# Layer 1's biases in its weights, one range check for four windows, logits in four key groups

## The chip, the cores and the metric

The kernel runs on one core of one Trainium2 chip. The metric is the device time of that core in microseconds, the median of several executions. The core has a matmul engine (TensorE, PE in the profile; PEld is its weight load), three engines for elementwise work (VectorE or DVE, ScalarE or ACT, GpSimd or POOL) and SyncE (SP), which here only issues DMA transfers. Matmuls read on-chip memory (SBUF) and write banks of PSUM, 128 partitions by 512 fp32 values, of which there are eight.

## The reference, cut to what matters

An image batch x of 4 x 128 channels x 64 x 64 goes through two layers.

```python
# layer 0, in windows of 16 x 16 pixels, BR = 2 branches, 4 heads of 32 channels
y = layernorm2d(x); y = y + depthwise_3x3(y)
q, k, v = (einsum('ncij,bhdc->nbhdij', windows(y), M) for M in (Wq, Wk, Wv))
logits = einsum('nbhdij,nbhdkij->nbhkij', q, patches_5x5(k)) * 32 ** -0.5   # zero padded
o = einsum('nbhkij,nbhdkij->nbhdij', softmax(logits, axis=3), patches_5x5(v))
x = x + unwindowed((Wo[0] @ o[0] + 0.5 * Wo[1] @ o[1]) / sqrt(1.25))

# layer 1, on tokens t: 4 x 4096 x 128
z = ln(t) @ W.T + b                     # W is 384 x 128; q, k, v are its thirds
q, k, v = elu(z_q) + 1, elu(z_k) + 1, z_v
t = t + (q . cumsum(k v^T)) / (q . cumsum(k) + 1e-6)
w = batchnorm(ln(t) @ Wf.T)
y_s = sigmoid(w_s + y_{s-1} @ V.T)      # a scan along the 4096 tokens
x = t + y
```

`ln` has no gain and no offset, so its output sums to zero over the 128 channels.

## The kernel before

The image is cut into 16 bands (4 images, 4 bands of 16 rows), a band into four windows, which makes 64 windows. The main loop (L708) walks one slot per window, with two slots more to drain. In slot i it writes, in this order: `logits` of window i, `scaled` (the division by the softmax sums) of window i-2, `weighted` of window i-1 (sums, values, inverse, in three steps) and `window_inputs` (q, k, v) of window i+1, in three steps. Between these stand six gaps (`between(i, 0)` to `between(i, 5)`); each takes one step of `behind`, the layer-1 work of a finished band (`layer1`, 24 steps in the list at L621, so one band of layer 1 per four slots), and in most slots one of `ahead`, the normalisation and depthwise convolution of a coming band. `in_order` (L161) fixes the order of PE, DVE, ACT and POOL to the written one; the SP queue takes its transfers in the order in which the Tile scheduler puts them, and a transfer into a buffer comes after the buffer's release. All PSUM tiles of this stage share eight banks.

**logits** (L371). For each head, a bank holds 128 key slots (partitions) by 512 queries (two branches of 256). A bf16 product of `mask_k` and `mask_q` (L379) first writes 0 or -1e30, then `BLOCKS` (L27) splits the queries into rows 0 to 6, 6 to 10 and 10 to 16, each with its own eight rows of keys (from rows 0, 4 and 8), in two halves of 64 key slots: 2 branches x 3 blocks x 4 heads x 2 halves = 48 products at L391, each with 32 rows (channels of the head) by 64 columns (keys) of the array, so eight tiles of it hold the 4 heads and 2 halves. ACT takes the exponentials `es` out of the banks (L400).

**weighted** (L403). A product with ones (L409) gives the sums `den`, and a transfer packs them into `dc` of 128 x 16; the values product (L421) uses `v_sb`, whose middle third is put together from the outer two by two transfers within SBUF (L360, L361). DVE adds the padding's share (L432), inverts (L434) and keeps a running maximum and minimum of the sums (L435, L436). These are compared with 1e-30 and 1e30 at the end (L876 to L879). If a sum left the range, or the recurrence's check failed, the program branches to `general`, another version of the whole computation.

**layer1** works on half bands of 512 tokens (16 x 2 of them). `turn` (L496) transposes the normalised tokens into `xl`. `feature` (L500), for q and for k, multiplies by a third of `awT`, takes exp(z + b) on ACT (L505), the minimum of this and 1 on DVE (L507) and then max(z + b + 1, that) on DVE (L508). `values` (L517) multiplies by the last third and adds `abv`, the bias spread over all partitions, on DVE (L528).

**prepare** (L134) runs once on DVE after the first convolutions and scales `woT`. After the main loop the recurrence (L823) runs 41 rounds and writes the output.

Of the kernel before, what the change touches and what calls it, by code (L numbers as in the profile page):

```python
# [9 lines left out]
F32 = mybir.dt.float32  # L10
BF16 = mybir.dt.bfloat16
AF = mybir.ActivationFunctionType
# [5 lines left out]
P = 128  # L18
# [5 lines left out]
BR, HEADS, HD = 2, 4, 32  # L24
KR = 2
KC = 64
BLOCKS = ((0, 6, 0), (6, 10, 4), (10, 16, 8))  # L27
BAND = WS * W
# [7 lines left out]
WARM = 11  # L36
TOL = 5e-7
TINY, HUGE = 1e-30, 1e30

# [8 lines left out]
def conv_attn_hybrid(ctx: ExitStack, tc: tile.TileContext, ins: dict, out: bass.AP):  # L48
# [75 lines left out]
    awT = loaded("awT", [P, 3 * P])  # L124
    ab = loaded("ab", [P, 3])
    abv = loaded("abv", [P, P], src=ins["abv"].partition_broadcast(P))
    fwT = loaded("fwT", [P, P])
# [3 lines left out]

    ab1 = const.tile([P, 2], F32, name="ab1")

    def prepare():  # L134


        rect = math.sqrt(1.0 + LAM * LAM * (BR - 1))
        nc.vector.tensor_scalar(woT[:, 0], woT[:, 0], 1.0 / rect, None, ALU.mult)
        nc.vector.tensor_scalar(woT[:, 1], woT[:, 1], LAM / rect, None, ALU.mult)
        nc.vector.tensor_scalar(ab1, ab[:, :2], 1.0, None, ALU.add)  # L140


    dmax = const.tile([P, 16], F32, name="dmax")
    nc.vector.memset(dmax, 1.0)
    dmin = const.tile([P, 16], F32, name="dmin")
    nc.vector.memset(dmin, 1.0)

# [32 lines left out]
    def run(g):  # L180
        for _ in g:
            pass
# [148 lines left out]
    def window_inputs(w, n, wj):  # L331
# [27 lines left out]

        nc.sync.dma_start(v_sb[:64, 1, :], v_sb[64:, 0, :])  # L360
        nc.sync.dma_start(v_sb[64:, 1, :], v_sb[:64, 2, :])  # L361
        w["v"] = v_sb
# [3 lines left out]

    def spans(br, n):
        r0, r1, key0 = BLOCKS[n]
        return slice(br * WT + r0 * WS, br * WT + r1 * WS), br * WT + key0 * WS

    def logits(w):  # L371
# [3 lines left out]
        for h in range(HEADS):  # L375
            rows = slice(h * HD, (h + 1) * HD)

            for c in range(0, P, KC):
# [6 lines left out]
                )  # L385
        for br, n in pieces:
            cols, k0 = spans(br, n)
            for h in range(HEADS):
                rows = slice(h * HD, (h + 1) * HD)
                for c in range(0, P, KC):  # L390
                    nc.tensor.matmul(  # L391
                        sps[h][c : c + KC, cols],
                        w["k"][rows, k0 + c : k0 + c + KC],
                        w["q"][rows, cols],
                        start=False,
                        stop=(br, n) == pieces[-1],
                    )
        for h in range(HEADS):
            es = p2.tile([P, BR * WT], F32, tag=f"es{h}", name=f"es{h}")
            nc.scalar.activation(es, sps[h], AF.Exp, scale=scale)  # L400
            w["es", h] = es

    def weighted(w):  # L403
# [8 lines left out]
        nc.scalar.copy(den, dps)  # L412
        dc = p2.tile([P, 16], F32, tag="dc", name="dc")
        nc.sync.dma_start(dc, den[::HD, :])
        yield
        for br, n in pieces:
            cols, _ = spans(br, n)
            for h in range(HEADS):
# [15 lines left out]
        nc.vector.reciprocal(rc, dc)  # L434
        nc.vector.tensor_tensor(dmax, dmax, dc, ALU.max)  # L435
        nc.vector.tensor_tensor(dmin, dmin, dc, ALU.min)  # L436
        rd = dram4.tile([HEADS, BR * WT], F32, tag="rd", name="rd")
# [58 lines left out]
    def turn(h):  # L496
        h.xl = p2.tile([P, 512], F32, tag="xl", name="xl")
        nc.scalar.copy(h.xl, turned(h.xn, 0, 4))

    def feature(h, m):  # L500

        zps = bank()
        nc.tensor.matmul(zps, awT[:, m * P : (m + 1) * P], h.xl, start=True, stop=True)  # L503
        low = p2.tile([P, 512], F32, tag="low", name="low")
        nc.scalar.activation(low, zps, AF.Exp, bias=ab[:, m : m + 1])  # L505
        f = p2.tile([P, 512], F32, tag=f"f{m}", name=f"f{m}")
        nc.vector.tensor_scalar(low, low, 1.0, None, ALU.min)  # L507
        nc.vector.scalar_tensor_tensor(f, zps, ab1[:, m : m + 1], low, ALU.add, ALU.max)  # L508
        return f
# [7 lines left out]
    def values(h):  # L517
        vvps = bank()
        for j in range(4):
# [7 lines left out]
        h.v1 = v1s[h.s]  # L527
        nc.vector.tensor_tensor(  # L528
            h.v1[:, :, :P],
            vvps.rearrange("p (j d) -> p j d", d=P),  # L530
            abv.unsqueeze(1).to_broadcast([P, 4, P]),
            ALU.add,
        )

# [160 lines left out]
    next(third)  # L695
    windows = {0: {}}
    run(window_inputs(windows[0], 0, 0))
# [3 lines left out]
    def between(i, gap):  # L701
# [3 lines left out]
        if i < len(places) and (i == 0 or i % NB or gap in (0, 2, 4)):  # L705
            next(ahead, None)

    for i in range(len(places) + 2):  # L708
        if i < len(places):
            n, wj = places[i]  # L710
            if i and wj == 0 and n + 1 < len(bands) and bands[n + 1][1] < NB - 1:
                load_head(n + 2)
            logits(windows[i])
        if 2 <= i:
            m, wjm = places[i - 2]
            if wjm == NB - 1:
                run(behind)
                behind = layer1(m, halves.pop(m - 1, (None, None)))
        between(i, 0)
        if 2 <= i:  # L720
            scaled(m, wjm, windows.pop(i - 2))
        if i < len(places) and wj == 1 and n + 2 < len(bands):
            load(n + 2)
        sums = weighted(windows[i - 1]) if 1 <= i <= len(places) else iter(())
        for gap in (1, 2):
            next(sums, None)
            between(i, gap)
        run(sums)
        if i == 0:
            run(fourth)  # L730
        inputs = iter(())
        if i + 1 < len(places):
            windows[i + 1] = {}
            inputs = window_inputs(windows[i + 1], *places[i + 1])
        for gap in (3, 4, 5):
            next(inputs, None)
            between(i, gap)
        run(inputs)
    run(behind)
# [119 lines left out]

    NG = 4  # L860
    okc = sp.tile([P, NG + 1], F32, name="okc")
    d = sp.tile([P, COLS], F32, name="d")
# [12 lines left out]

    nc.vector.tensor_scalar(dmax, dmax, HUGE, None, ALU.is_le)  # L876
    nc.vector.tensor_scalar(dmin, dmin, TINY, None, ALU.is_ge)
    nc.vector.tensor_tensor(dmin, dmin, dmax, ALU.mult)
    nc.vector.tensor_reduce(okc[:, NG : NG + 1], dmin, AX.X, ALU.add)  # L879
    okp = ps_m.tile([P, 512], F32, tag="bank", name="bank")  # L880
    nc.tensor.matmul(okp[:1, : NG + 1], ones[:, :1], okc, start=True, stop=True)
    oks = sp.tile([1, 1], F32, name="oks")
    nc.vector.tensor_reduce(oks, okp[:1, : NG + 1], AX.X, ALU.add)
    bad = sp.tile([1, 1], mybir.dt.int32, name="bad")
    nc.vector.tensor_scalar(bad, oks, float(2 * P * B * SEGS + P * 16), None, ALU.is_lt)
    rec.close()
# [591 lines left out]
def _masks():  # L1478
# [10 lines left out]
    pad = np.zeros((1, BR, WT), np.float32)  # L1489
    for r0, r1, key0 in BLOCKS:  # L1490
        for q in range(r0 * WS, r1 * WS):
            r, c = divmod(q, WS)
            for i in range(8):
                queries[:, i, :, q] = 0.0 if abs(key0 + i - r) <= KR else -BIG
            for j in range(WS):
# [60 lines left out]
```

## Time and profile before

| | us |
|---|---|
| median of 3 runs | 928.18 (926.36 to 929.19) |
| the profiled execution | 923.71 |
| its span | 922.0 |
| PE busy | 871.1 (94%) |
| PEld busy | 647.3 (70%) |
| DVE busy | 737.1 (80%) |
| ACT busy | 539.9 (59%) |
| POOL busy | 256.4 (28%) |
| L391, logits: PE busy, 6144 passes | 90.7 |
| L400, exponentials, ACT, x256 | 132.2 |
| L508, feature, DVE, x64 | 48.0 |

An fp32 matmul shows as two passes, each with its own weight load. A pass is counted once per tile of the array, and passes of several tiles run side by side, so that busy time is the union and a mean is not a cost. The span is the time between the first and the last instruction that the profiler saw; the execution's own time has 1.7 us more around it. Times in microseconds from the start of the span are used below to name places.

### The profile page before, as it was taken

To read this page: it belongs to the slowest core of one execution; us is meant where nothing else is said; L and a number is where in the kernel's file an instruction comes from. 1 tells how busy PE (TensorE), PEld (TensorE's weight loads), DVE (VectorE), ACT (ScalarE), POOL (GpSimd) and SP (SyncE) were. 2 spreads that over 40 slices of the span, in tenths; PEclk is the share of its full clock that TensorE was granted. 3 is DMA by queue.
4 is the path that set the end of the run, shared out by engine and by line. 5 is a ranking of instruction groups with operands and counts; after the bars stand their busy time and mean duration, and the time that the engine had idled before them with its cause. 6 is when DMAs were issued, how large, how long until landed. Compare 5 with 4: busy or idle time off the path is not lost.

```text
span 922.0 us, 33116 instructions
## 1 busy us (share of the span) xinstructions
PE 871.1 (94%) x13836; PEld 647.3 (70%) x13836; DVE 737.1 (80%) x2408; ACT 539.9 (59%) x1010; POOL 256.4 (28%) x358
## 2 busy tenths in 40 slices
PE   4977999999999999999999999999999999978885
PEld 3756777777777877777787777777777778656452
DVE  6464878888898978798888889787978887577695
ACT  3754666565756565665656575656666565522563
POOL 2122131423232232304132323323231412131174
PEclk9989999999999999999999999999999999989798
DMA  4111121122222121212112121212121111110854
GB/s 122 35 46 55 38 79 42 50 58 64 61 64 55 53 57 50 75 38 71 49 50 61 61 60 50 63 50 68 50 72 38 57 39 51 43 37 23 365 212 159
DMA packets 53071, 63.89 MB, mean 69 GB/s; under 512 B 22960, under 2 KB 33840, under 8 KB 52400
## 3 DMA queue, kind: packets, MB, share of 16 engines
q1 hardware_dynamic: 51184, 56.91, 19.8%
q10 hardware_dynamic: 1728, 4.77, 1.3%
q8 instruction: 111, 1.82, 0.8%
q14 instruction: 48, 0.39, 0.1%
HBM read 35.44 MB, written 17.30 MB: 57 GB/s over the span
## 4 chain that ended last, share of the span: by engine, by line
PE 59%; DVE 26%; DMA 4%; ACT 4%; issue 3%; POOL 2%; ACTq 0%; DVEq 0%; SPq 0%; POOLq 0%
DVE y L289 9%; PE bank L338 8%; PE bank L474 7%; PE bank L213 6%; PE bank L391 6%; PE bank L503 5%; PE bank L409 4%; PE bank L351 4%; PE bank L421 3%; PE bank L611 3%; DMA res<-resd 2%; DVE st L192 2%; PE bank L546 2%; PE z L831 2%; DVE state L571 2%
## 5 line engine op out<-in xcount | busy, mean ns | idle before, releaser
L289 DVE SCALAR_TENSOR_TENSOR y<-ypad,cpe_w,y 128x512 f32<-128x512 f32 x240 | 190.1, 792 | 14.5 <-ACT y L287 11.0
L400 ACT ACTIVATE es<-bank 128x512 f32<-128x512 f32 x256 | 132.2, 603 | 64.5 <-PE bank L391 64.5
L449 POOL TENSOR_TENSOR oT<-o_sb,rden 128x512 f32<-128x512 f32 x64 | 85.0, 1328 | 240.0 <-DMA rden<-rd 166.5
L196 POOL TENSOR_SCALAR rs<-mv 128x4 f32<-128x4 f32 (+2 forms) x100 | 25.2, 252 | 366.0 <-DVE mv L194 162.5
L204 DVE TENSOR_SCALAR xn<-x,mv,rs 128x128 f32<-128x128 f32 x256 | 92.5, 422 | 26.6 <-POOL rs L197 26.6
L197 POOL TENSOR_TENSOR rs<-rs,mhalf 128x4 f32<-128x4 f32 (+2 forms) x100 | 106.1, 1061 | 8.3
L391 PEld LDWEIGHTS bank<-q,k 32*64 32x64 f32 x6144 | 89.1, 132 | 4.4 <-ACT k L346 1.8
L391 PE MATMUL bank<-q,k 32*64 32x96 f32 (+1 forms) x6144 | 90.7, 247 | 1.0 <-ACT k L346 1.0
L421 PEld LDWEIGHTS bank<-es,v_sb 128*32 128x32 f32 x3072 | 56.5, 110 | 30.7 <-issue 19.5
L474 PE MATMUL bank<-woT,oT 128*128 128x128 f32 x512 | 67.3, 287 | 7.5 <-POOL oT L449 7.5
L474 PEld LDWEIGHTS bank<-woT,oT 128*128 128x128 f32 x512 | 64.0, 200 | 11.6 <-POOL oT L449 9.2
L421 PE MATMUL bank<-es,v_sb 128*32 128x96 f32 (+1 forms) x3072 | 69.9, 239 | 0.5 <-issue 0.5
L503 PE MATMUL bank<-xl,awT 128*128 128x512 f32 x128 | 70.0, 630 | 0.0
L358 ACT COPY v_sb<-bank 128x512 f32<-128x512 f32 x64 | 37.5, 586 | 54.1 <-PE bank L351 46.0
L409 PE MATMUL bank<-es,ones 128*32 128x512 f32 x512 | 69.0, 611 | 0.0
L338 PE MATMUL bank<-y2w,wqT 128*128 128x256 f32 x256 | 67.0, 385 | 1.0 <-DVE y2w L289 1.0
L338 PE MATMUL bank<-y2w,wkT 128*128 128x256 f32 x256 | 65.8, 380 | 0.0
L351 PE MATMUL bank<-wvT,y2w 128*128 128x256 f32 x256 | 65.8, 380 | 0.0
L346 ACT COPY q<-bank 128x512 f32<-128x512 f32 x64 | 37.6, 587 | 44.2 <-PE bank L338 42.1
L346 ACT COPY k<-bank 128x512 f32<-128x512 f32 x64 | 37.3, 583 | 36.8 <-PE bank L338 36.7
L192 DVE BATCH_NORM_STATS2 st<-x 128x6 f32<-128x128 f32 x256 | 55.5, 279 | 1.1
L338 PEld LDWEIGHTS bank<-y2w,wqT 128*128 128x128 f32 x256 | 46.2, 195 | 13.0 <-issue 7.2
(118 smaller groups left out, 1719.6 us busy)
## 6 DMA issues: line engine op xcount, KB each, us to landing
rden<-rd SPq DMA_DIRECT2D x64, 256.0 KB
v_sb<-v_sb SPq DMA_DIRECT2D x128, 64.0 KB
resd<-rs_o SPq DMA_DIRECT2D x32, 256.0 KB
out<-ot SPq DMA_DIRECT2D x32, 256.0 KB
xin<-in_xt SPq DMA_DIRECT2D x15, 512.0 KB
res<-resd SPq DMA_DIRECT2D x2, 2048.0 KB
res<-resd ACTq DMA_DIRECT2D x2, 2048.0 KB
dc<-den SPq DMA_DIRECT2D x64, 8.0 KB
```

What stands on the lines that cost most here:

```text
L197: nc.gpsimd.tensor_tensor(rs[:, :n], rs[:, :n], mhalf[:, :n], ALU.pow)
L204: nc.vector.tensor_scalar(xn[:, j, :], piece, mv[:, j, 0:1], rs[:, j : j + 1], ALU.subtract, ALU.mult)
L289: nc.vector.scalar_tensor_tensor(y2, src, cpe_w[:, tap : tap + 1], y2, ALU.mult, ALU.add)
L338: nc.tensor.matmul(pps[:, br * WT : (br + 1) * WT], wT[:, br * P : (br + 1) * P], y2, start=True, stop=True,)
L351: nc.tensor.matmul(vps[:, e * 256 : (e + 1) * 256], y2[:, e * P : (e + 1) * P], wvT, start=True, stop=True,)
L391: nc.tensor.matmul(sps[h][c : c + KC, cols], w["k"][rows, k0 + c : k0 + c + KC], w["q"][rows, cols], start=False, stop=(br, n) == pieces[-1],)
L400: nc.scalar.activation(es, sps[h], AF.Exp, scale=scale)
L409: nc.tensor.matmul(dps[rows], ones[:, :HD], w["es", h], start=True, stop=True)
L421: nc.tensor.matmul(ops[rows, cols], w["v"][:, n, c0 : c0 + HD], w["es", h][:, cols], start=(br, n) == pieces[0], stop=(br, n) == pieces[-1],)
L449: nc.gpsimd.tensor_tensor(oTs[n][:, :, :, wj * WS : (wj + 1) * WS], w["o"].rearrange("p (a r c) -> p a r c", a=BR, c=WS), w["rden"].rearra ...
L474: nc.tensor.matmul(yps[:, j * P : (j + 1) * P], oT[:, br, t], woT[:, br, :], start=br == 0, stop=br == BR - 1,)
L503: nc.tensor.matmul(zps, awT[:, m * P : (m + 1) * P], h.xl, start=True, stop=True)
```

## The change

Layer 1's biases: `ab` is now all 384 biases, spread over all partitions. `prepare` computes the sums of `awT` over its 128 rows on TensorE, adds 1 to the biases of q and k, and adds (bias - sum) / 128 to every row of `awT`, so that each of its columns sums to the bias. `turn` adds 1 to `xl` while it evicts it. As `ln`'s output sums to zero over the channels, the product then holds z + b (+ 1 for q and k) by itself. `feature` takes exp(that - 1), with a constant column `minus` as bias, and one DVE instruction makes max(min(low, 1), product). `values` evicts with a copy on ACT.

The sums' range: `dc` is a quarter of a tile for four windows. In the fourth window, `in_range` makes two DVE instructions over 64 columns, which count the sums in range into a column of `okc`. `dmax` and `dmin` are gone.

The logits: the middle block's halves hold key rows 8 to 12 and 4 to 8, so the first half of the key slots always holds rows 0 to 4 or 8 to 12 and the second rows 4 to 8 or 12 to 16. Per branch there are two steps instead of three blocks: rows 0 to 4 for queries of rows 0 to 6 beside rows 4 to 8 for 0 to 10, and rows 8 to 12 for 6 to 16 beside rows 12 to 16 for 10 to 16. That is 32 products of 96 or 160 columns. `mask_q` and the transfers of `v_sb`'s middle third follow.

The slot's order is written as a list; what it orders is as before, but for `load` (the band's input transfer), which is now written right behind `logits`, ahead of `between(i, 0)` and `scaled`.

```diff
-BLOCKS = ((0, 6, 0), (6, 10, 4), (10, 16, 8))
+BLOCKS = ((0, 6, (0, 4)), (6, 10, (8, 4)), (10, 16, (8, 12)))
+TILES = (((0, 0, 0, 6), (1, 4, 0, 10)), ((0, 8, 6, 16), (1, 12, 10, 16)))
...
-    ab = loaded("ab", [P, 3])
-    abv = loaded("abv", [P, P], src=ins["abv"].partition_broadcast(P))
+    ab = loaded("ab", [P, 3 * P], src=ins["ab_all"].partition_broadcast(P))
...
-        nc.vector.tensor_scalar(ab1, ab[:, :2], 1.0, None, ALU.add)
+        sums = bank()[:, : 3 * P]
+        nc.tensor.matmul(sums, ones, awT, start=True, stop=True)
+        nc.vector.tensor_scalar(ab[:, : 2 * P], ab[:, : 2 * P], 1.0, None, ALU.add)
+        nc.vector.tensor_tensor(ab, ab, sums, ALU.subtract)
+        nc.vector.scalar_tensor_tensor(awT, ab, 1.0 / P, awT, ALU.mult, ALU.add)
...
-        nc.sync.dma_start(v_sb[:64, 1, :], v_sb[64:, 0, :])
-        nc.sync.dma_start(v_sb[64:, 1, :], v_sb[:64, 2, :])
+        nc.sync.dma_start(v_sb[:64, 1, :], v_sb[:64, 2, :])
+        nc.sync.dma_start(v_sb[64:, 1, :], v_sb[64:, 0, :])
...
-        for br, n in pieces:
-            cols, k0 = spans(br, n)
-            for h in range(HEADS):
-                rows = slice(h * HD, (h + 1) * HD)
-                for c in range(0, P, KC):
-                    nc.tensor.matmul(
-                        sps[h][c : c + KC, cols],
-                        w["k"][rows, k0 + c : k0 + c + KC],
-                        w["q"][rows, cols],
...
+        for br in range(BR):
+            for step in TILES:
+                for h in range(HEADS):
+                    rows = slice(h * HD, (h + 1) * HD)
+                    for half, key, r0, r1 in step:
+                        cols, k0 = span(br, r0, r1), br * WT + key * WS
+                        nc.tensor.matmul(
+                            sps[h][half * KC : (half + 1) * KC, cols],
+                            w["k"][rows, k0 : k0 + KC],
+                            w["q"][rows, cols],
...
+    def in_range(group):
+        found = dens.pop(group).rearrange("p w e -> p (w e)")
+        low = p1.tile([P, DGROUP * 16], F32, tag="low_dc", name="low_dc")
+        nc.vector.tensor_scalar(low, found, HUGE, None, ALU.is_le)
+        nc.vector.scalar_tensor_tensor(
+            low, found, TINY, low, ALU.is_ge, ALU.mult, accum_out=okc[:, NG + group : NG + group + 1]
+        )
...
-        nc.vector.tensor_tensor(dmax, dmax, dc, ALU.max)
-        nc.vector.tensor_tensor(dmin, dmin, dc, ALU.min)
+        if at == DGROUP - 1:
+            in_range(group)
...
-        nc.scalar.copy(h.xl, turned(h.xn, 0, 4))
+        nc.scalar.activation(h.xl, turned(h.xn, 0, 4), AF.Identity, bias=ones[:, :1])
...
-        nc.scalar.activation(low, zps, AF.Exp, bias=ab[:, m : m + 1])
+        nc.scalar.activation(low, zps, AF.Exp, bias=minus)
         f = p2.tile([P, 512], F32, tag=f"f{m}", name=f"f{m}")
-        nc.vector.tensor_scalar(low, low, 1.0, None, ALU.min)
-        nc.vector.scalar_tensor_tensor(f, zps, ab1[:, m : m + 1], low, ALU.add, ALU.max)
+        nc.vector.scalar_tensor_tensor(f, low, 1.0, zps, ALU.min, ALU.max)
...
-        nc.vector.tensor_tensor(
-            h.v1[:, :, :P],
-            vvps.rearrange("p (j d) -> p j d", d=P),
-            abv.unsqueeze(1).to_broadcast([P, 4, P]),
-            ALU.add,
-        )
+        nc.scalar.copy(h.v1[:, :, :P], vvps.rearrange("p (j d) -> p j d", d=P))
```

## The prediction

> **What bounds the kernel now.** I read the busy time of each engine in stretches of 47 us first, because an average over the span mixes three stages.
>
> ```profile
> core 0: us, PE busy (x) PEld busy (x) DVE busy (x) ACT busy (x) POOL busy (x), PEclk, DMA share, GB/s
> ...
> 228.00:275.00 47.00, 46.95 (x791) 35.08 (x790) 40.78 (x140) 28.70 (x52) 12.97 (x19) 1.00 0.18 54
> ...
> 416.00:463.00 47.00, 46.97 (x830) 35.40 (x831) 40.26 (x125) 30.01 (x55) 12.21 (x17) 1.00 0.21 61
> ...
> 792.00:850.00 58.00, 49.28 (x482) 37.58 (x480) 41.12 (x155) 18.61 (x32) 10.99 (x15) 0.94 0.11 36
> 850.00:922.00 72.00, 55.31 (x181) 29.79 (x180) 50.94 (x92) 35.81 (x90) 30.79 (x35) 0.86 0.60 235
> ```
>
> From about 90 to 810 us TensorE is busy 46.9 of every 47 us at the full granted clock, DVE 40, ACT 29. One band of 16 rows takes about 47 us and four slots, so a slot is 11.7 us of TensorE work in the written order. TensorE time saved there comes off the end, as long as DVE and ACT stay under it. From 810 to 850 the last band's layer 1 runs alone, and after 850 the recurrence, which the change leaves as it is.
>
> Next the TensorE timeline of one slot's start and, from the chain of waits, undisturbed groups (start, duration, line; x counts passes, two for each fp32 matmul).
>
> ```profile
> 406.92 0.42 PE L379 MATMUL bank<-mask_q,mask_k 32*64 32x512 bf16 x8
> 407.16 1.39 PE L391 MATMUL bank<-q,k 32*64 32x96 f32 x96
> 408.48 0.49 PE L582 MATMUL bank<-v,aT 128*128 128x129 f32 x2
> ```
>
> ```profile
> 416.85 0.86 PE bank L338 x4
> ...
> 423.98 1.00 PE bank L409 x8
> ...
> 426.47 1.02 PE bank L421 x48
> ```
>
> The logits of a window (L391) hold TensorE from 407.16 to 408.48: 1.32 us. L338 streams 4 passes of 256 columns in 0.86 us, 0.84 ns for a column and pass.
>
> **The logits.** Eight tiles of the array (four heads, two key halves) each stream 2 branches x 256 query columns, twice: 1024 x 0.84 = 0.86 us when all run abreast. This doesn't change: 96+64+96 columns per branch become 96+160 in one half and 160+96 in the other. So 0.46 of the 1.32 us is not streaming. L409 and L421 stream as much in each of their four tiles and take 1.00 and 1.02 us, so some 0.15 us belongs to any such group (the change-over to the next shape), and 0.31 us comes with L391's number of matmuls. It falls from 48 to 32 a window (96 to 64 passes). Bounds: if the 0.31 us shrinks with the count alone, a third goes, 0.10 us; if it vanishes, 0.31 us. I take the count's place between the rows: 48 passes (L421) cost nothing extra, 96 cost 0.31, so 64 keep a third and 0.20 us goes. Over 64 windows: **-12.8 us** (-6.4 to -19.8).
>
> The Trainium skill (TensorE: Matmul & The Clock Gate, "Architectural detail") gives TensorE a queue of 64 instructions. A matmul of two passes is four instructions (two weight loads, two passes), so by that rule a third of a window's 192 can wait in line before, half of 128 after, and weight loads would be fetched ahead more often: a gain nearer the upper bound. No row shows the queue, and the sum doesn't use it.
>
> **DVE's work.** The rows of the groups by form:
>
> ```profile
> L507 DVE TENSOR_SCALAR low<-low 128x512 f32<-128x512 f32 x64 | 27.4, 428 | 26.8 <-ACT low L505 26.7
> L528 DVE TENSOR_TENSOR v<-bank,abv 128x512 f32<-128x512 f32 x32 | 21.9, 683 | 0.7 <-PE bank L520 0.6
> L436 DVE TENSOR_TENSOR dmin<-dmin,dc 128x16 f32<-128x16 f32 x64 | 10.4, 162 | 0.0
> L435 DVE TENSOR_TENSOR dmax<-dmax,dc 128x16 f32<-128x16 f32 x64 | 7.1, 111 | 0.0
> L346 ACT COPY q<-bank 128x512 f32<-128x512 f32 x64 | 37.6, 587 | 44.2 <-PE bank L338 42.1
> ```
>
> Gone: the minimum L507 (27.4; the fused L508 does it in its own 751 ns), the value addition L528 (21.9), the two running extremes (17.5): 66.8 us. New: one range check for four windows, 16 x (two operations on 128x64, taken as 0.25 us each, between the 0.16 us of L436 on 16 columns and the 0.62 us of L866 on 256, and an accumulator read of 0.08 us) = 9 us. Net -57 us, 3.6 us a band: DVE goes from 40 to about 36.5 of the band, now some 46. DVE is not the last to be done in these stretches, so this work is worth only the waits that it ends. TensorE's waits for DVE between 40 and 790 us are 1.9 us at transposes (L213 waiting for x of L596), and 5.4 us in its weight loads there: I take -1.0 us (0 to -5).
>
> In the last band DVE is the chain:
>
> ```profile
> 830.38 0.34 DVE low L507
> ...
> 831.50 0.35 DVE low L507
> ...
> 835.51 0.44 DVE low L507
> ...
> 836.72 0.60 DVE v L528
> ```
>
> These four go: **-1.7 us** (0, if ACT or TensorE is right behind, to -3.1, all four minima of 0.43 and both additions of 0.68). L876 to L879, 0.7 us in all, lie beside TensorE work near 810 us: 0.
>
> **ACT's work.** The values' 32 evictions move to ACT: 32 x 0.59 (row L346, the same copy out of PSUM) = 19 us, and the 32 evictions of `xl` get a bias, 593 to some 690 ns (row L505, 688 ns, an activation with a bias): 3 us. ACT goes from 29 to 30.5 of a band; TensorE's 46 hide it. In a slot they stand at gap 4 (half 0) and gap 3 (half 1), where `k` or `v` of the next window is queued behind; these are needed only at the next slot's logits or later. 0; with the cover gone up to 19 us (a rival below).
>
> **Start.** `prepare` gains a 128x384 product on TensorE (2 x 384 x 0.84 = 0.65 us) and about 1.3 us on DVE (two operations on 384 columns, one on 256, by the 0.79 us of L289 on 512). TensorE is free from 12.36 (the end of L213's 0.47 us from 11.89) to 13.59, where L307 waits for the padded rows, and `awT` has landed by 9.96 us in the packet records. DVE does `prepare` at 22.3 us, the normalised rows that follow have over 2 us of slack before their transposes at 29.69, and then it sits idle 9.24 us until 36.92. Cost 0, with the cover gone +2. The bias row's 192 KB in place of 64 KB has ten us to arrive.
>
> **Queues.** SP issues the same transfers. Its `load` is written ahead of `between(0)` and `scaled`, but the buffer it fills is free only after L481 of the second half, at 433.89 in that slot, and the load leaves at 434.59, behind that window's `rd` and `rden`. It can't go ahead of the `dc` transfer: DVE needs `dc` at 431.30, before that L481, so the two would wait for each other. 0. The two `v_sb` transfers keep bytes and count, and now stay in their own 64 partitions: 0.
>
> Sum: 12.8 + 1.0 + 1.7 = 15.5 us off the profiled execution's span of 922.0 (923.71 with what lies around it), so 906.5 and 908.2. The three timed runs have their median at 928.18, 4.5 above that execution; the same difference carries it to **912.7 us**.
>
> **Rivals.**
> (a) *The unequal halves pace each other.* If matmuls start and end in the written order, a 96-column tile waits for the 160-column one beside it, and every step costs 160: 4 x 160 x 2 x 0.84 = 1.08, with the 0.15 of change-over 1.23 us. Gain 0.09 x 64 = 5.8, with 2.7 from DVE 8.5: 919.7 us. For: all eight tiles now have equal work in every step, so the trace can't show the case. Against: up to 32 of L391's passes touch one tenth of a microsecond, so the tiles overlap freely. Chance 0.17. The Trainium skill (TensorE: Matmul & The Clock Gate, "The mechanism" of Part 3) states this rule: matmuls are strict first in, first out, at start and end. The trace's records carry no tile, so they neither confirm nor refute it.
> (b) *The count is not the cost.* If the 0.31 us is the price of eight row-and-column tiles (as against four), the logits stay at 1.32 us: only 2.7 us go, 925.5. For: no group in this trace has eight fp32 tiles with fewer matmuls. Chance 0.10.
> (c) *Everything beyond streaming goes*: 19.8 + 2.7 = 22.5, 905.7. Chance 0.06.
> (d) *ACT takes the lead; slower.* At gaps 3 and 4 ACT would evict late, a bank come free late and TensorE stand, 0.59 us in each of 32 halves: +19 - 15.5 = +3.4, 931.6. It decides from 0.48 us exposed per half. Against: ACT is idle 18 of 47 us, waiting for TensorE at these very copies (44 us before L346's q). Chance 0.05.
> The forecast keeps 0.62.
>
> The range takes the logits' bounds and DVE's: 22.5 to 27 us off at the low end, 6 to 8 at the high: 902 to 923. It holds the forecast, (a) and (c); (b), (d) and part of the forecast's edges are left out. A run set tells 0.3% (2.8 us, 925.4) from no change; (b) lies on that edge and is split: faster 0.89, same 0.06, slower 0.05.
>
> **What would show it.** After: L391 with 4096 passes, and from its start to the next group's 1.12 us (1.23 for (a), 1.32 for (b), 1.01 for (c)); TensorE still busy 99% from 90 us on, in bands of about 46 us; DVE near 680 us in sum, ACT near 562; no new wait of TensorE for ACT at the banks of L338 or L520 (else (d)); the stretch from 829 to 838 shorter by about 2 us. The prediction is wrong if TensorE shows idle time in the steady bands, whichever engine ends it.

## The result, and the profile after

| | before | after |
|---|---|---|
| median, us | 927.27 (4 runs, 925.18 to 929.19) | 904.72 (4 runs, 902.29 to 906.12) |
| the profiled execution | 923.71 | 903.84 |
| its span | 922.0 | 902.1 |

The ratio of the times is 0.9744, with a 95% interval of 0.9712 to 0.9775 (the two medians divided give 0.9757). The kernel became 22.55 us faster by the medians and 19.9 by the two profiled spans; the forecast was 15.5.

The busy times of the page of after, and then the engines' shares of the chain that ended last, first of after and then of before:

```profile
PE 852.1 (94%) x11790; PEld 634.3 (70%) x11790; DVE 686.5 (76%) x2229; ACT 561.5 (62%) x1042; POOL 256.1 (28%) x358
...
PE 75%; DVE 11%; DMA 5%; ACT 3%; POOL 2%; issue 2%; ACTq 0%; SPq 0%; POOLq 0%; DVEq 0%
```

```profile
PE 59%; DVE 26%; DMA 4%; ACT 4%; issue 3%; POOL 2%; ACTq 0%; DVEq 0%; SPq 0%; POOLq 0%
```

TensorE's share of busy time is 94% in both, but DVE's share of the chain fell from 26% to 11%. The prediction didn't read the shares of the chain; the 26% was the warning that it missed (the share is 27% in e1 below, which keeps DVE's old work, and 9% in e2, which doesn't).

The groups of the page of after that answer to the changed lines (logits; `low`; the fused `f`). Line numbers are those of after: the mask product is L385, the logits L398, the transposes L220, the q product L345, the states L586, x L611, the range check L416 and L417.

```profile
L528 DVE SCALAR_TENSOR_TENSOR f<-low,bank 128x512 f32<-128x512 f32 x64 | 43.6, 682 | 49.5 <-ACT low L526 49.5
...
L398 PE MATMUL bank<-q,k 32*64 32x96 f32 (+1 forms) x4096 | 77.4, 276 | 1.0 <-ACT k L353 1.0
...
L526 ACT ACTIVATE low<-bank,minus 128x512 f32<-128x512 f32 x64 | 44.1, 689 | 19.2 <-PE bank L524 19.2
```

There are 4096 passes in place of 6144. The 49.5 us of idle time before the fused operation will matter below: DVE stands there, waiting for ACT's exponential.

TensorE's timeline of after around one window's logits (start, duration, line, passes):

```profile
397.54 0.42 PE L385 MATMUL bank<-mask_q,mask_k 32*64 32x512 bf16 x8
397.77 1.20 PE L398 MATMUL bank<-q,k 32*64 32x96 f32 x64
398.90 0.49 PE L597 MATMUL bank<-v,aT 128*128 128x129 f32 x2
```

From the logits' start to the next group it is 1.13 us; the median over the steady windows is 1.125, against 1.318 before. That is 0.193 us a window, 12.4 us over 64 windows, where the forecast said 12.8. The rest of the gain is elsewhere. A band is four slots, and the mask product marks where a slot starts. These are the busy times of one band's four slots, before and then after (length of the slot, then each engine's busy time):

```profile
406.92:421.33 14.41, 13.92 (x229) 11.14 (x229) 13.72 (x60) 7.33 (x14) 4.86 (x7) 1.00 0.17 53
421.33:434.66 13.33, 13.33 (x228) 10.74 (x228) 10.42 (x43) 8.31 (x16) 4.20 (x8) 1.00 0.18 53
434.66:446.23 11.57, 11.57 (x193) 7.31 (x193) 9.83 (x27) 7.98 (x15) 3.41 (x3) 1.00 0.31 83
446.23:457.35 11.12, 11.12 (x207) 8.57 (x206) 9.65 (x18) 7.70 (x14) 1.75 (x1) 1.00 0.14 39
```

```profile
397.54:410.68 13.14, 13.14 (x198) 10.93 (x198) 12.23 (x57) 7.31 (x14) 4.87 (x7) 1.00 0.21 61
410.68:423.81 13.13, 13.13 (x195) 10.53 (x194) 10.27 (x41) 8.32 (x16) 4.20 (x8) 1.00 0.18 51
423.81:435.14 11.33, 11.33 (x161) 7.07 (x160) 9.83 (x24) 8.78 (x16) 3.40 (x3) 1.00 0.33 83
435.14:446.07 10.93, 10.93 (x175) 8.38 (x174) 7.44 (x14) 8.18 (x15) 1.27 (x1) 1.00 0.14 39
```

Slots 1, 2 and 3 became 0.19 to 0.24 shorter, which is the logits' share. Slot 0 became 1.27 shorter here. Before, DVE was busy 13.72 of its 14.41 us: it set this slot's length, though over the band it was busy only 43.6 of 50.4. TensorE's timeline shows where it waited in that slot, before and then after:

```profile
412.67 1.16 PE L546 MATMUL bank<-f,f 128*128 128x128 f32 x8
413.67 0.38 PE L213 MATMUL bank<-ident,x 128*128 128x128 f32 x2
414.50 0.59 PE L213 MATMUL bank<-ident,x 128*128 128x128 f32 x2 [0.46 <-DVE x L596]
414.93 1.03 PE L338 MATMUL bank<-y2w,wqT 128*128 128x256 f32 x4
```

```profile
403.10 1.16 PE L561 MATMUL bank<-f,f 128*128 128x128 f32 x8
404.09 0.60 PE L220 MATMUL bank<-ident,x 128*128 128x128 f32 x4
404.53 1.03 PE L345 MATMUL bank<-y2w,wqT 128*128 128x256 f32 x4
```

From the first transpose of x to the q product it took 1.26 us before and takes 0.44 after: 0.82 us of standing, of which the row shows 0.46 as idle. The remainder lies under the transposes' own records and is counted as busy. This is one of the longer waits: over the 12 steady bands (those of the last table below) the stretch took 0.97 us on average before, from 0.59 to 1.40, and takes 0.44 after, so 0.53 us a band is gone here. The Trainium skill (Perfetto Trace Analysis, "Tensor Engine Instruction (MATMUL, LD_WEIGHTS)") says that a TensorE record's end is estimated and not observed; these rows agree, and show how much of a wait that can cover.

Later in the same slot TensorE stands once more, at the transposes of xn, the normalised tokens that DVE writes. Before and then after, DVE's row first:

```profile
419.01 1.11 DVE L204 TENSOR_SCALAR xn<-x,mv,rs 128x128 f32<-128x128 f32 x4
...
419.50 1.00 PE L213 MATMUL bank<-ident,xn 128*128 128x128 f32 x4
420.34 0.39 PE L582 MATMUL bank<-v,aT 128*128 128x129 f32 x2
```

```profile
408.36 1.11 DVE L211 TENSOR_SCALAR xn<-x,mv,rs 128x128 f32<-128x128 f32 x4
...
408.91 0.95 PE L220 MATMUL bank<-ident,xn 128*128 128x128 f32 x4
409.69 0.39 PE L597 MATMUL bank<-v,aT 128*128 128x129 f32 x2
```

Four such passes took 0.44 us at x after; from these to the next product it is 0.84 us before and 0.78 after, on average 0.83 and 0.71, while DVE is still writing xn. No row shows idle time for it. So the changed kernel still stands here for some 0.27 us a band.

The lag can be seen on DVE. Its timeline in the same slot, before and then after; the last rows of after are the range check:

```profile
405.45 0.68 DVE L528 TENSOR_TENSOR v<-bank,abv 128x512 f32<-128x512 f32 x1
...
407.50 1.33 DVE L571 TENSOR_TENSOR state<-state,bank 128x129 f32<-128x129 f32 x4
...
414.10 0.61 DVE L596 SCALAR_TENSOR_TENSOR x<-bank,rd,x 128x128 f32<-128x128 f32 x2
```

```profile
396.28 1.33 DVE L586 TENSOR_TENSOR state<-state,bank 128x129 f32<-128x129 f32 x4
...
402.88 0.61 DVE L611 SCALAR_TENSOR_TENSOR x<-bank,rd,x 128x128 f32<-128x128 f32 x2
...
406.44 0.13 DVE L416 TENSOR_SCALAR low_dc<-dc 128x64 f32<-128x64 f32 x1
406.61 0.23 DVE L417 SCALAR_TENSOR_TENSOR low_dc<-dc,low_dc 128x64 f32<-128x64 f32 x1
406.76 0.08 DVE L417 DVE_READ_ACCUMULATOR low_dc<-dc,low_dc 128x1 f32 x1
```

The state additions started 0.58 us after the slot's mask product before (407.50 against 406.92), and start 1.26 us ahead of it now (396.28 against 397.54). DVE enters slot 0 with 1.8 us less work left over, so x is there when TensorE comes to its transposes.

The whole difference by place, from the starts of the 64 mask products (means over the 12 steady bands; my own sums):

```
             slot 0  slot 1  slot 2  slot 3 | to 13th mask | 48 steady slots | next three | last mask to end | span
before        14.07   13.42   11.53   11.12 |    155.63    |     601.66      |   36.96    |     127.72       | 921.98
after         13.01   13.27   11.33   10.93 |    154.29    |     582.55      |   36.39    |     128.88       | 902.11
difference    -1.06   -0.15   -0.20   -0.19 |     -1.34    |     -19.11      |   -0.57    |      +1.16       | -19.87
```

Of the 19.1 us in the steady slots, 48 x 0.193 = 9.3 is the logits and 9.8 is slot 0 standing less, 0.8 us for each of 12 bands: 0.53 at the transposes of x and 0.26 from the v product ahead of the transposes of xn to the product behind them. This split is by place; what each half of the change is worth by itself is another question, and the experiments answer it.

### The profile page after: what moved, and what is told of

It reads as the page before. It is cut to its first block, busy times and chain, and to the rows that moved or that the text cites. A ratio compares the mean times of both kernels' runs of the same rounds, so it can differ in the third digit from the quotient of the medians.

```text
span 902.1 us, 28877 instructions
## 1 busy us (share of the span) xinstructions
PE 852.1 (94%) x11790; PEld 634.3 (70%) x11790; DVE 686.5 (76%) x2229; ACT 561.5 (62%) x1042; POOL 256.1 (28%) x358
## 4 chain that ended last, share of the span: by engine, by line
PE 75%; DVE 11%; DMA 5%; ACT 3%; POOL 2%; issue 2%; ACTq 0%; SPq 0%; POOLq 0%; DVEq 0%
PE bank L345 11%; PE bank L524 7%; PE bank L495 7%; PE bank L398 6%; PE bank L427 6%; PE bank L220 6%; PE bank L442 6%; PE bank L358 5%; PE bank L561 3%; PE bank L626 3%; PE bank L597 3%; PE bank L540 3%; DVE y L296 3%; DMA res<-resd 3%; PE bank L578 2%; PE bank L599 2%
## 5 line engine op out<-in xcount | busy, mean ns | idle before, releaser
L296 DVE SCALAR_TENSOR_TENSOR y<-ypad,cpe_w,y 128x512 f32<-128x512 f32 x240 | 186.7, 778 | 11.7 <-ACT y L294 7.5
L470 POOL TENSOR_TENSOR oT<-o_sb,rden 128x512 f32<-128x512 f32 x64 | 82.3, 1285 | 229.0 <-DMA rden<-rd 192.7
L211 DVE TENSOR_SCALAR xn<-x,mv,rs 128x128 f32<-128x128 f32 x256 | 94.5, 430 | 28.2 <-POOL rs L204 28.2
L528 DVE SCALAR_TENSOR_TENSOR f<-low,bank 128x512 f32<-128x512 f32 x64 | 43.6, 682 | 49.5 <-ACT low L526 49.5
L398 PEld LDWEIGHTS bank<-q,k 32*64 32x64 f32 x4096 | 75.7, 132 | 4.4 <-ACT k L353 1.8
L398 PE MATMUL bank<-q,k 32*64 32x96 f32 (+1 forms) x4096 | 77.4, 276 | 1.0 <-ACT k L353 1.0
L442 PEld LDWEIGHTS bank<-es,v_sb 128*32 128x32 f32 x3072 | 56.5, 110 | 30.1 <-issue 26.2
L345 PE MATMUL bank<-y2w,wqT 128*128 128x256 f32 x256 | 67.2, 386 | 1.5 <-DVE y2w L296 1.5
L345 PE MATMUL bank<-y2w,wkT 128*128 128x256 f32 x256 | 66.1, 381 | 0.0
L526 ACT ACTIVATE low<-bank,minus 128x512 f32<-128x512 f32 x64 | 44.1, 689 | 19.2 <-PE bank L524 19.2
```

The costliest lines, as they stand in the source:

```text
L211: nc.vector.tensor_scalar(xn[:, j, :], piece, mv[:, j, 0:1], rs[:, j : j + 1], ALU.subtract, ALU.mult)
L296: nc.vector.scalar_tensor_tensor(y2, src, cpe_w[:, tap : tap + 1], y2, ALU.mult, ALU.add)
L345: nc.tensor.matmul(pps[:, br * WT : (br + 1) * WT], wT[:, br * P : (br + 1) * P], y2, start=True, stop=True,)
L398: nc.tensor.matmul(sps[h][half * KC : (half + 1) * KC, cols], w["k"][rows, k0 : k0 + KC], w["q"][rows, cols], start=False, stop=br == BR - ...
L442: nc.tensor.matmul(ops[rows, cols], w["v"][:, n, c0 : c0 + HD], w["es", h][:, cols], start=(br, n) == pieces[0], stop=(br, n) == pieces[-1],)
L470: nc.gpsimd.tensor_tensor(oTs[n][:, :, :, wj * WS : (wj + 1) * WS], w["o"].rearrange("p (a r c) -> p a r c", a=BR, c=WS), w["rden"].rearra ...
```

## The experiments

The expectations use letters. **A**: TensorE sets slots 1 to 3, and DVE's left-over work sets slot 0; so a saving on TensorE is lost in slot 0 as long as DVE is late there, and a saving on DVE is paid in slot 0. **B**: TensorE bounds every slot, and each part is worth what it saves there. **Q**: a matmul of the logits is held up because TensorE holds only so many instructions, which enter in the written order and are freed in order; the eight array tiles themselves run independently of each other. Other letters in them are rivals whose price stands beside them; (a) to (d) are those of the prediction. "Steady slots" are those of the last table.

**Each half of the change by itself.** `e1_logits_only` is the kernel before with the new `BLOCKS`, `TILES`, masks and transfers; `e2_rest_only` is the changed kernel with the 48 products of before.

```diff
 # e1, on the kernel before; e2 is the reverse, on the changed one
-BLOCKS = ((0, 6, 0), (6, 10, 4), (10, 16, 8))
+BLOCKS = ((0, 6, (0, 4)), (6, 10, (8, 4)), (10, 16, (8, 12)))
+TILES = (((0, 0, 0, 6), (1, 4, 0, 10)), ((0, 8, 6, 16), (1, 12, 10, 16)))
...
-        for br, n in pieces:
+        for br in range(BR):
+            for step in TILES:
```

> The kernel before with the logits in 32 products and nothing else. Measured between the two traces: a window's logits took 1.318 us before and 1.125 after, and nearly every slot is 0.19 us shorter, but the first slot of each band (window 0) is shorter by a further 0.9 us; there DVE was busy 13.4 of 14.1 us before. Theory A (DVE sets the end of that slot before): with TensorE 0.19 us quicker in every slot and DVE's work unchanged, TensorE reaches its transposes of x earlier and waits longer; what three of a band's four slots gain is lost in the first slot. The logits take 1.125 us a window, but the kernel gains only 3 to 8 us against before, and slot 0 of a band gets longer by 0.2 to 0.6 us. Theory B (parts add up): 64 x 0.193 = 12.4 us gained.

> The changed kernel with the logits again in 48 products: biases in the weights, values evicted by ACT, range check for four windows. Theory A (DVE's backlog held TensorE in the first slot of each band): these slots lose 0.8 to 0.9 us each, 13 bands, so 10 to 12 us are gained against before, and 11 to 13 us are lost against the change; the sum of this gain and that of the logits alone is well under 22.5. Theory B (parts add up): 22.5 - 12.4 = 10 gained. The prediction's own terms for this part: 2.7.

Beside the kernel before at 927.06 us, e1 took 923.18 (ratio 0.9956, 0.9935 to 0.9976) and e2 909.22 (0.9816, 0.9783 to 0.9848). So the logits alone give 3.9 us, as A said, although their group became shorter by the same 0.19 us as in the whole change. TensorE's timeline of e1 in slot 0:

```profile
414.86 0.38 PE L214 MATMUL bank<-ident,x 128*128 128x128 f32 x2
415.83 0.59 PE L214 MATMUL bank<-ident,x 128*128 128x128 f32 x2 [0.59 <-DVE x L597]
416.25 0.60 PE L339 MATMUL bank<-y2w,wqT 128*128 128x256 f32 x2
```

The stretch that took 1.26 us before takes 1.39 here (0.97 and 1.43 on average over the steady bands): TensorE comes earlier and waits longer. Steady slots 1 to 3 are 0.15 to 0.20 shorter than before and slot 0 is 0.21 longer (14.28), so a band gains 0.33 of its 4 x 0.193 us. DVE's work alone, in e2, shortens slot 0 to 12.97 and no other slot: 1.12 us a band, 13.5 over the twelve.

e2's 17.8 us is more than any theory said. Its profiled span is 15.9 us shorter than that of before: the steady slots give 13.5, the stretch up to the 13th mask product gives 4.3, and the end takes 1.9 back. The unaltered kernel below shows that the place of the 4.3 moves between executions of one kernel. The two parts' gains add up (3.9 + 17.8 = 21.7, against 22.55), where A expected a sum well under that. By bands they nearly add as well: 0.33 + 1.12 = 1.45 of 1.59 us.

Against the changed kernel, A expected e2 to lose 11 to 13 us. In the steady slots it loses 5.6 us to after, and 7.2 to e8, which is the same kernel once more. That is what the new logits are worth with DVE's work already moved: 0.47 to 0.60 us a band, not their 4 x 0.193 = 0.77. Slot 0 is the reason: it is 12.97 us with the old logits and 12.89 to 13.02 with the new ones. In e2 TensorE hardly stands at the transposes of xn (0.47 us to the next product); in the change it comes earlier and stands there.

**The number of products, and their order.** `e3_even_steps` has the same 32 products, but in each step both halves have 96 or both 160 columns; `e4_forty_products` has two steps in one branch and three in the other.

```diff
 # e3
+STEPS = (((0, 0, 0, 6), (1, 12, 10, 16)), ((0, 8, 6, 16), (1, 4, 0, 10)))
+TILES = (STEPS, STEPS[::-1])
 # e4
+TILES = (
+    (((0, 0, 0, 6), (1, 4, 0, 10)), ((0, 8, 6, 16), (1, 12, 10, 16))),
+    (((0, 0, 0, 6), (1, 4, 0, 6)), ((0, 8, 6, 10), (1, 4, 6, 10)), ((0, 8, 10, 16), (1, 12, 10, 16))),
+)
```

> The changed kernel with the same 32 products in another order: a step's two halves have the same length (96 and 96, or 160 and 160), short, long, long, short. Theory Q (TensorE holds 64 instructions in the written order and frees them in that order; a model of it gives 1.32 us for 48 products and 1.12 for 32, as measured): 1.08 us a window, 0.04 less, so 2.7 us gained against the change. Rival (a) of the prediction in a milder form (unequal halves pace each other, 160 for each step): 128 columns x 2 x 0.84 = 0.21 us less, up to 13 us gained. Theory C (only the count of products matters): 1.125 us, no change.

> The changed kernel with one branch's 160-column products split in two (96 and 64): 40 products. Theory Q: 1.25 us a window, so 8 us slower than the change. Theory C, by the straight line of the prediction between 48 and 96 passes, drawn through what was measured (64 passes 1.125, 96 passes 1.318): 80 passes 1.22 us, 6 us slower. Theory D (it is the 64-column pieces that cost, not the count): half of the way as well, 1.22. If the first slot of a band stays free of waits, the slots all lengthen by the same amount.

e3 took 903.07 us (0.9748, 0.972 to 0.9776), e4 909.2 (0.9821, 0.9787 to 0.9856). Their timelines of TensorE, e3 and then e4, logits and the group behind:

```profile
311.86 1.15 PE L399 MATMUL bank<-q,k 32*64 32x96 f32 x64
312.94 0.70 PE L221 MATMUL bank<-ident,x 128*128 128x128 f32 x4
```

```profile
312.54 1.31 PE L401 MATMUL bank<-q,k 32*64 32x96 f32 x80
313.78 0.66 PE L223 MATMUL bank<-ident,x 128*128 128x128 f32 x4
```

Start to start it is 1.08 us in e3 and 1.24 in e4 (medians 1.080 and 1.244 to 1.249). With 48, 40 and 32 products a window's logits take 1.318, 1.245 and 1.125 us: the cost goes with the count, and the second eight products fewer are worth more than the first. The number of 64-column pieces goes with the count in these three (theory D), and no run separates the two; the order of the same 32 products is worth 0.045 us more (e3). In time, the 2.7 us that Q expected of e3 aren't seen: its ratio is that of the change, and in the steady slots it gains 0.7 us on after and loses 0.9 to e8. e4 is 3.1 to 4.7 us slower there than the two, where Q's 8 us for the whole run would be 6; slots 2 and 3 lengthen by 0.12 to 0.14, slot 1 by 0.05, slot 0 not at all.

If unequal halves paced each other step by step, as rival (a) had it, evening them out would save 4 x 160 x 2 x 0.84 - 0.86 = 0.22 us; it saved 0.045. Q named 1.08 and 1.25 beforehand. It is an estimate from a small model with 64 instructions held (four for an fp32 matmul) and the other constants fitted on the trace of before, where it gives 1.32; the model's working isn't shown here. The 64 is the Trainium skill's (TensorE: Matmul & The Clock Gate, "Architectural detail"); these four values agree with it (1.32 and 1.12 were known to the model, 1.08 and 1.25 weren't) and no row shows the queue itself. The Trainium skill (TensorE: Matmul & The Clock Gate, "The mechanism" of Part 3) has matmuls end strictly in the written order, which by the prediction's reading would make the logits 1.23 us; the measured 1.125 us, and the 0.045 us between the two orders, don't agree with that reading. The records carry no tile, so the order of the ends itself can't be read from them.

**Which of DVE's savings counts.** Three kernels each put one piece of DVE's work back into the changed one; `e8_change_again` is the changed kernel unaltered, for the spread between executions.

```diff
 # e5
-        nc.scalar.copy(h.v1[:, :, :P], vvps.rearrange("p (j d) -> p j d", d=P))
+        nc.vector.tensor_copy(h.v1[:, :, :P], vvps.rearrange("p (j d) -> p j d", d=P))
 # e6, ahead of the fused operation
+        nc.vector.tensor_scalar(low, low, 1.0, None, ALU.min)
 # e7, beside the range check
+        nc.vector.tensor_tensor(dmax, dmax, dc, ALU.max)
+        nc.vector.tensor_tensor(dmin, dmin, dc, ALU.min)
```

> The changed kernel with the values evicted by a copy on DVE instead of ACT (the bias stays in the weights): 32 x 0.68 us more on DVE, two in a band, one of them near the end of its third quarter. The runs so far show that the first slot of a band (window 0) carries DVE's lag: 14.07 us before, 13.01 with the change, 14.28 with the logits alone, while the other three slots follow TensorE. Theory A (lag: only DVE work that is not yet worked off when that slot begins counts): slot 0 grows by 0.3 to 0.7 us and no other, 4 to 9 us over 13 bands. Theory P (in proportion: the rest of the change took 57 us off DVE and gave some 15): 22 x 15 / 57 = 6 us, in any slot. Rival (d) of the prediction, that ACT has a price: the kernel gets faster, or slots 2 and 3 shorter.

> The changed kernel with the minimum of exp and 1 again as a DVE instruction of its own ahead of the fused one (which then does it a second time, to no effect): 64 x 0.43 = 27 us more on DVE, four in a band, in slots 2 and 3, the last at step 14 of 24, early in slot 3. DVE is idle 1.6 us of slot 2 and 3.5 of slot 3. Theory A: most is worked off there; slot 0 grows by 0 to 0.3 us, 0 to 4 us in all. Theory P: 27 x 15 / 57 = 7 us. The last band's layer 1, where DVE is alone, gets up to 1.7 us longer in both.

> The changed kernel with the running maximum and minimum of the sums computed beside the check for four windows (their result isn't used): 128 x 0.14 = 17.5 us more on DVE, 0.27 in every slot. Theory A: slot 0 has it within its own chain of DVE work and grows by 0.25 to 0.5 us, the others stay: 3 to 6 us. Theory P: 17.5 x 15 / 57 = 4.6 us.

> The changed kernel once more, beside these three on the same chip, for the differences to it, and to see how far parts that wait for transfers move from one execution to the next: the slot of the pipeline's filling that took 25.7 us before and between 22.5 and 28.9 in the five other traces, and the stretch from the last window's mask to the end (125.2 to 129.7). If these belong to the kernel, they come out as in its first trace (28.0 and 128.9) within 0.3 us; if they belong to the execution, they differ by a microsecond or more. The steady slots are expected within 0.1 us of the first trace.

The kernel before took 923.39 us here, e8 899.77 (0.9751, 0.9726 to 0.9775). The others:

```
                   median   ratio (95%)               slot 0  slot 1  slot 2  slot 3
e8 unaltered       899.77   0.9751 (0.9726, 0.9775)    12.89   13.26   11.33   10.93
e5 values on DVE   909.39   0.9865 (0.984, 0.989)      13.43   13.27   11.33   10.93
e6 minimum         908.5    0.9832 (0.9804, 0.986)     13.43   13.27   11.33   10.93
e7 extremes        903.88   0.9798 (0.9775, 0.9821)    13.11   13.27   11.33   10.93
```

All three lengthen slot 0 and leave the other three where they are. Against e8 the growths are 0.54, 0.54 and 0.22 us, together 1.30; e1, which has all of DVE's old work with the new logits, has 14.28 - 12.89 = 1.39. But slot 0 of the unaltered kernel is itself 12.89 to 13.02 us in its three traces; against the longer one the growths are 0.41, 0.41 and 0.09, together 0.91 of 1.26. So the three parts make up most of slot 0's loss, and the extremes' part is hardly clear of the spread. Moving the values to ACT is a clear gain, 4.9 to 6.5 us in the steady bands, and rival (d) falls with it. Theory P is right in size for the first two (6 and 7 us named for the whole run; 4.9 to 6.5 and 5.0 to 6.6 measured in the steady slots; for the extremes 4.6 named and 1.2 to 2.8 measured) but not in place, since it had no reason for one slot alone. A had the place of the minimum right, and its size wrong: it expected next to nothing, since DVE has idle time in the later slots to work a lag off. The groups of e6 show where that idle time stands:

```profile
L528 DVE TENSOR_SCALAR low<-low 128x512 f32<-128x512 f32 x64 | 28.1, 439 | 35.4 <-ACT low L526 35.3
```

DVE waits for ACT's exponential and only then does the minimum. This wait is ahead of the work: it can take up a lag from before, but not the minimum behind it, which moves what follows on DVE. DVE's wait for this exponential is 49.5 us in after and 35.4 here, so a part of the 28.1 us is worked off and a part reaches slot 0. That is argued from the two rows; no run moved the minimum to another place.

e8 against after: the steady slots agree within 0.12 us, yet the spans differ by 4.1. The slot from the sixth to the seventh mask product is 28.03 us in after and 25.96 in e8; in the chain of waits it hangs on transfers of `dc` and `rden` of 4 to 5 us each. In e11 below, the unaltered kernel a third time, it is 23.76. e2's is 22.46 and before's 25.67. With 23.8 to 28.0 us in three executions of one kernel, that place belongs to the execution, not to the kernel, and with it most of e2's surplus.

**What is left in slot 0.** DVE is still busy 12.23 of 13.14 us in slot 0 of after, and the range check, 0.44 us, stands in that slot. `e9_check_two_slots_later` moves it to slot 2; `e10_both` adds e3's order; `e11_change_third` is the changed kernel for the same chip, where the kernel before took 927.84 us.

```diff
-        if at == DGROUP - 1:
-            in_range(group)
+        if at == 1 and group or group == NR - 1 and at == DGROUP - 1:
+            in_range(group if at > 1 else group - 1)
```

> The changed kernel with a group's range check two windows later (in the third slot of a band instead of the first; the last group's where it was). In the change's trace the check's two DVE instructions and the accumulator read (0.13, 0.23 and 0.08 us) stand in the first slot of each band, the one in which TensorE waits for DVE. Theory A (DVE's lag in that slot): slot 0 shorter by 0.1 to 0.3 us (12.89 and 13.01 us in two executions of the change), no other slot longer, 1 to 4 us in all. Theory P (DVE's sum counts): the work is the same, no change.

> The changed kernel with the range check two windows later and the logits in even steps (short, long, long, short). The logits take 1.08 us a window (as with even steps alone), slots 1 to 3 are 0.045 us shorter, slot 0 by as much as DVE lets it: 2 to 2.9 us from the logits, 1 to 4 from the check, 3 to 6 us faster than the change. If DVE's lag takes back in slot 0 what the logits give, 1 to 3.

> The changed kernel on the same chip, as the base for these two. Steady slots within 0.1 us of its first two traces (slot 0 13.01 and 12.89 us, the others 13.27, 11.33, 10.93); the filling slot and the end are left open.

```
                   median   ratio (95%)               slot 0  slot 1  slot 2  slot 3   sum
e11 unaltered      902.98   0.973  (0.9704, 0.9755)    13.02   13.27   11.33   10.93   48.55
e9 check moved     901.58   0.9722 (0.9698, 0.9746)    12.79   13.23   11.33   10.93   48.28
e10 and even steps 898.82   0.9677 (0.9652, 0.9702)    12.73   13.20   11.29   10.89   48.11
```

Moving the check shortens slot 0 by 0.23 us against e11, 3.2 over the 48 steady slots, but by 0.10 against e8; the medians show 1.4, within the intervals' overlap. The transposes of xn fit: to the next product it is 0.48 us in e9, and 0.57 to 0.71 in the three traces of the unaltered kernel. So A's direction is borne out, and the gain in time isn't shown. In e3 alone, slot 0 gained nothing (13.05); with the check out of the way, e10's four slots together are 0.44 us shorter than e11's and 0.3 shorter than e8's. e10 is 4.2 us faster than the change beside it and the fastest version found.

## Why the prediction was right or wrong

**The logits: the group right, its worth not.** The step "64 keep a third and 0.20 us goes" measured 0.193 us, and L398's 4096 passes and 1.125 us are the numbers named for it. The count's place between the two rows was a guess that 40 products would have bent: they cost 1.245, not the 1.22 half-way. What wasn't seen is that this saving is paid only while DVE is not late: by itself it is worth 3.9 us (e1), and beside the rest of the change 5.6 to 7.2 us of the steady slots' 9.3.

**DVE's relief: the term that was mis-sized.** The text took "-1.0 us (0 to -5)" because "DVE is not the last to be done in these stretches". In slots 1 to 3 that holds; in slot 0 it doesn't. The relief is worth 13.5 us over the 12 steady bands without the new logits (before to e2) and 15.2 with them (e1 to after); by place, 9.8 us of the pair's difference is slot 0 standing less. Two steps of the reading failed. The stretches of 47 us averaged over the kernel's own period: a band lasts 50.1 us, not "about 47", and has one slot in which DVE is busy 95%. And the price was taken from the idle column, 1.9 us at the transposes of x, which appears there in four slots only and showed 0.46 of a stall of 0.82 us in the one above; the mean stall there was 0.53 us in each of 12 bands, 6.4 us, and those at xn showed nowhere. The "46.9 of every 47" was a reading of the fullest rows as well: between 87 and 745 us the stretches of before show 46.15 to 46.97.

**The sign named for being wrong.** It was idle time of TensorE in the steady bands. The view of waits shows 1.4 us between 90 and 775 us of after, for POOL, but by the starts of the groups TensorE stands some 0.27 us a band at xn, so the sign was one that this profile can't show. The bands last 48.55 us, not the "about 46" named.

**DVE's work: nearly right.** The page's busy time fell from 737.1 to 686.5 us, 50.6 less for the 57 expected; overlapping records count once in it, and the groups' own times added up fall by 68.0. The range check costs 16 x 0.44 = 7.0 us for 9. The fused operation fell from 751 to 682 ns, 4.4 us in all, which wasn't foreseen.

**The last band: not resolved.** From the last mask product to the issue of the load that opens the recurrence, 59.2 us became 57.9: 1.3 less, of which 0.19 is the last window's logits, so 1.1 for the 1.7 taken. But the stretch takes 58.2 and 58.8 us in the other two traces of the unaltered change, and 56.5 in e1, which still has the four DVE steps. So a term of this size isn't shown either way. The chain of waits of after has TensorE where the four DVE steps stood, which was the case of the lower bound:

```profile
809.66 1.01 PE bank L524 x2
810.67 0.89 PE bank L561 x8
811.56 0.86 PE bank L524 x2
812.42 0.44 PE bank L553 x4
```

In this pair the recurrence took it back: from its first to its last output addition it lasts 36.7 us before and 37.8 after, and 36.7 to 39.3 over all the traces.

**ACT, start and queues at nothing: right as far as the runs show.** ACT is at 561.5 us (562 was named), TensorE waits 1.0 us for its `k` at the logits in sum, as before, and the view of waits shows none at the banks of q, k, v and the values. The first mask product starts at 23.51 us, for 23.40 before, with the new product of `prepare` ahead of it. Nothing in the first slots stands out from the spread that e8 and e11 show there.

**The rivals.** (a) would have shown 1.23 us, (b) 1.32, (c) 1.01: all refuted by 1.125, and (a)'s mechanism by e3. (d) is refuted by e5. The time came out near (c)'s 905.7 by another way. The forecast's 912.7 lies 8.0 us above the median, within its range; the DVE term went beyond even its bound of 5 us, and the range held only because it also covered 19.8 us for the logits. That is luck in part: two terms were off in opposite directions. The logits' 12.8 us was some 5 to 9 too much (they are worth 3.9 us by e1, and 6 to 8 by the ratios of e2 and of the three runs of the change), and DVE's 1.0 more than 12 too little (13.5 in the steady slots of e2).

**What stays open.** Whether the queue's length, rather than something else that grows with the number of products, makes the 0.31 us isn't shown, only that a model with it hits two values named beforehand. Whether the count of the products or the 64-column pieces among them is the cost isn't separated. What sets the length of the slot from the sixth to the seventh mask product in an execution wasn't tried.

## What to carry to other kernels

Read busy shares by the kernel's own period, slot by slot: an engine at 87% over a band can be at 95% in one slot, and there a part of its work is paid in time (in e5 to e7, 0.09 to 0.54 us of slot 0 for 1.1 to 1.8 us of DVE work a band) while a part of the saving on the engine at "99%" is lost (more than half of it in e1). Where an engine seems never idle, compare the starts of the same groups from slot to slot, since the modelled ends hide a wait. Idle time that an engine spends waiting doesn't take up work queued behind that wait; periodic work belongs in a slot whose slack comes after it (argued from e6 and e9, whose gain in time is within the spread).

## What the hardware showed unexpectedly

The order of the same 32 products alone changes a window's logits from 1.125 to 1.080 us. The fused max of DVE takes 682 ns with a constant and its PSUM operand second, against 751 with a per-partition operand and PSUM first; which of these differences does it wasn't separated, and the first operation changed with them, from an addition to a minimum. A stall of TensorE of 0.82 us appeared as 0.46 us of idle time, and the stalls at the transposes of xn, some 0.27 us a band in after, as none.
